# The bound check ahead of the pairs, the first batch's finish a pair earlier, and other moves in a written order

## The chip, the cores and the metric

The kernel runs on one core of a Trainium2 chip. The metric is the device time of one execution in microseconds (us); a kernel is judged by the median of its runs. "Clock" is the mean clock that the throttle granted to TensorE over the span, as a share of full speed.

The engines are named as the profile names them: PE is TensorE's matmul side and PEld its weight load, DVE is VectorE, ACT is ScalarE, POOL is GpSimd, SP is SyncE, which in this kernel issues most DMAs. "ACT's queue" or "POOL's queue" are DMAs that those engines issue.

## The reference, cut to what matters

x is 2 x 512 x 64 x 32 in fp32: two images with 512 channels and S = 2048 tokens. Two layers follow one another, all in fp32.

```python
# layer 0: attention over all 2048 tokens, 8 heads of 64
qk = concat([x, freq_and_time_embedding], channels)       # 512 + 64 channels
q, k, v = qk @ Wq, qk @ Wk, x @ Wv
o = softmax(q k^T / 8) v                                   # per head, 2048 x 2048
x1 = o @ Wout + bout + x

# layer 1: Nystroem attention, 256 landmarks, 8 heads of 64
q, k, v = layernorm(x1) @ Wqkv                             # q scaled by 1/8
qL, kL = mean of q, k over groups of 8 tokens              # 256 landmarks
attn1, attn2, attn3 = softmax(q kL^T), softmax(qL kL^T), softmax(qL k^T)
z = attn2^T / (max column sum * max row sum of attn2)      # maxima over all heads and images
6 times: xz = attn2 z; z = z (13 - xz (15 - xz (7 - xz))) / 4
t = x1 + (attn1 (z (attn3 v)) + conv33(v)) @ Wout + bout   # conv over 33 tokens, per head
out = t + layernorm(t) @ W_nf4^T @ W^T                     # W_nf4: 4-bit weights, dequantised
```

Note the scale of z: it needs attn2 of every head and image, so no pseudo-inverse can begin before the last head's attn2 is there.

## The kernel before, in words

**Who sets the order.** The program is one function, fast_path, under a manual schedule: PE, DVE, ACT and POOL each carry out their instructions in the order in which the Python code emits them. Only SP's queue is ordered by the scheduler. Overlap is made by emitting pieces of one piece of work between pieces of another: such a piece of work is a generator, `advance(gens, n)` takes n steps from a list of generators, and a step that yields GAP takes a turn without emitting anything (the next generator in the list gets the turn instead). So the place of each `yield` and each `gap(n)` is a place in the engines' queues. A token block is 512 tokens, four per image; channels are four chunks of 128.

**Opening.** Twenty warm-up matmuls (L848) keep PE busy while the first weights, the embedding and x arrive. The class Heads0 prepares a pair of heads of layer 0: for queries and for keys a small matmul makes the embedding's part (frequency row plus time row), one 128 x 2048 addition on POOL (L889) sums the two into an e tile, and the projections (L902) are evicted with e added (L905).

**Layer 0.** attention0 handles eight pairs of heads one after the other, four per image. Per group of steps it emits scores (L1066), exps (L1074), additions of the exps (L1084) and values (L1096). Beside it run generators that make the next pair's keys, queries and values, and, during the first pairs of the second image, finish0_units for the first image: per token block an output projection with residual (L965, evicted in L972), a mean over channels by matmul (L987, from L984), a subtraction (L988), squares on ACT (L991, L994), additions on DVE (L996, L997), a variance matmul (L1000), a square-root (L1002) and the normalised block, written to DRAM as x_hat. At the end of an attention a loop runs until the one generator that the next attention needs is finished:

```python
            if not group:
                while needed in filler:
                    advance(filler)
```

`advance(filler)` takes the steps from the front of the list, so other generators in it run too, until the needed one is done.

**Layer 1, first pass.** keys_and_queries (L1239) projects x_hat; per pair, attend makes attn2 (the landmark products L1280 and their exps L1287) for its two heads, and gram (L1307) the start of the pseudo-inverse. In all pairs but the last, attend's two heads share one score tile, sc2, of two banks: the exp of the first head reads it before the second head's product writes its own half. Sixteen small memsets of ones columns (L1275) run on POOL. After the last pair's attend, start_scale (L1191 to L1196) makes zs, the common scale of all pseudo-inverses.

**Layer 1, second pass.** A loop runs over eight pairs, `todo`: the four of image 1, then the four of image 0. In each of its turns pinv of the pair runs, with three others woven into it. The pseudo-inverse of both heads is five iterations of flips (L1522, transposes) and products (L1532) with DVE subtractions (L1545), then three narrow products ending in u (L1507, L1516). After each iteration `chunk(c)`, c = 0 to 4, is called, and six times in the end part `last(i)`. In chunk(c), c = 0 to 3, stand

- attn1 of the pair before, token block c: scores (L1589), exps (L1594), the sum of the two exps (L1598), values in PSUM bank av1 (L1605), row sums over partitions (attn1_sums: matmuls L779 into rs and an ACT copy L1613), the inverse (attn1_inverse: DVE reciprocal L1618 and `spread`, eight SP DMAs, L790, that bring rinv to all partitions), and, one chunk later, the end: av1 times rinv on DVE (L1625), added into o on POOL (L1626);
- attn3 of the pair after, steps 2c and 2c + 1: scores (L1361), exps (L1370), additions (L1375), values (L1382).

chunk(4) has the 33-tap convolution of the next pair (L1459), and the values of the pair after that (L950) go into the `last` steps.

**Finish of layer 1.** Finish1 handles one token block: its x1 comes back from DRAM by four SP loads of 256 KB (L1637); then the output projection (L965, evicted in L972), statistics as above, a DVE reciprocal of the deviation (L1650), the folded feed-forward map mT (L1682), its scaling and residual (L1671, L1672) and a store (L1673). For image 1, finish1_units is a generator over four blocks; it is put into the list `finish` when the loop's fifth turn (n == NPAIR) has ended, and its steps are taken wherever chunk and last call `advance(finish)`. All its blocks share one xr buffer, xb_g, so a block's load waits for the stores of the block before.

**Tail.** After the loop, attn1 of the last pair (last_attn1), what remains of image 1's finish and the first two blocks of image 0's finish are emitted by a string with one letter per step:

```python
    for c in "f1f1f1f1f1f1f1fa1a1a1as11bs1bs1bbt":
```

f is a step of image 1's finish, 1 of last_attn1, a and b of the two blocks' output projections, s and t of their statistics. Then comes the bound check: a matmul bp_f (L2058) of a half-and-half matrix, halves_f, set by three POOL memsets (L2054 to L2056), small DVE operations and an all-reduce over partitions on POOL (L2064). Its flag decides, after the fast path, whether a general path runs instead. The feed-forward maps fp_g of image 0's four blocks (L1682) follow; wide_banks puts them alternately into product banks and the side banks av1 and av3.

Of the kernel before, what the change touches and what calls it, by code (L numbers as in the profile page):

```python
# [663 lines left out]
def fast_path(  # L664
# [157 lines left out]
    nc.vector.memset(emb_sb, 0.0)  # L822
# [3 lines left out]
    def load_w0(kind, cols, queue=nc.sync):  # L826
        w = {"q": wq0, "k": wk0}[kind]
        nc.sync.dma_start(w_sb[kind][:, :, cols], chunked(w[:C, cols]))
        queue.dma_start(we[kind][:, cols], w[C:, cols])

    nc.gpsimd.dma_start(emb_sb[:32, :H], freq)
    nc.gpsimd.dma_start(emb_sb[32:, H:], time)
    load_w0("q", slice(0, P), nc.scalar)

# [23 lines left out]
    class Heads0:  # L858
# [12 lines left out]
        def embedded_and_projected(self, kind):  # L871
# [5 lines left out]
            def embedded(kind):  # L877


                e = wpool0.tile([P, H, W], F32, tag="e", name=f"e_{kind}_{self.name}")  # L880
                flat, kept = e.rearrange("p h w -> p (h w)"), e_d["qk".index(kind), self.hp]
                if self.b:
                    nc.sync.dma_start(flat, kept)
                    return flat
                fp = bank(f"fp_{kind}_{self.name}")
                nc.tensor.matmul(fp[:, : H + W], lhsT=we[kind][:, cols], rhs=emb_sb, start=True, stop=True)
                ft = wpool0.tile([P, H + W], F32, tag="ft", name=f"ft_{kind}_{self.name}")
                nc.vector.tensor_copy(ft, fp[:, : H + W])
# [91 lines left out]
    def statistics(xb, xn, part, name, squares, row):  # L980
# [73 lines left out]
    def attention0(hd, filler, n_filler, needed, beside=None, every=False):  # L1054
# [62 lines left out]
        for i in range(0, len(steps) + 1, GROUP):  # L1117
# [13 lines left out]
            if not group:  # L1131
                while needed in filler:
                    advance(filler)
# [74 lines left out]
    class Pair:  # L1208
# [419 lines left out]
    class Finish1:  # L1628
# [13 lines left out]
        def steps(self, row):  # L1642
# [5 lines left out]
            for rstd in statistics(self.xb, self.xn, self.xn[:, :2, :], self.name, squares, row):  # L1648
# [236 lines left out]
    todo[1].prefetch_w()  # L1885
    vals = [values(1)]
    advance(vals)
    for n in todo[NPAIR - 1].front():
        advance(vals, n // 2)
    start_scale()  # L1890
    todo[0].prefetch1(kvpool.tile([P, S], F32, tag="k", name="q2_first"))
# [4 lines left out]
    for n, pair in enumerate(todo):  # L1896
# [122 lines left out]
    fs = [last_block(t) for t in range(NTB)]  # L2019

# [5 lines left out]

    outs = [f.out_units() for f in fs]
# [9 lines left out]
    st = [f.steps(deviation_of(t)) for t, f in enumerate(fs)]  # L2037

    ones_last = last_attn1()
    for c in "f1f1f1f1f1f1f1fa1a1a1as11bs1bs1bbt":  # L2040
        if c == "f":
            advance(finish)
        else:
            next({"1": ones_last, "a": outs[0], "b": outs[1], "s": st[0], "t": st[1]}[c])
# [5 lines left out]

    n = 3 * B * NPAIR

    halves = row_of("halves_f")[:, :P]
    nc.gpsimd.memset(halves, 0.0)  # L2054
    nc.gpsimd.memset(halves[:D, :D], 1.0)
    nc.gpsimd.memset(halves[D:, D:], 1.0)  # L2056
    bp = bank("bp_f")
    nc.tensor.matmul(bp[:, :n], lhsT=halves, rhs=bound, start=True, stop=True)  # L2058
    ok = small.tile([P, n], F32, name="ok_f")
    nc.vector.tensor_scalar(ok, bp[:, :n], SAFE, None, ALU.is_lt)  # L2060
    oks = small.tile([P, 1], F32, name="oks_f")
    nc.vector.tensor_reduce(oks, ok, AX.X, ALU.min)
    nc.vector.tensor_scalar(oks, oks, -1.0, 1.0, ALU.mult, ALU.add)
    nc.gpsimd.partition_all_reduce(bad, oks, P, bass_isa.ReduceOp.max)  # L2064

# [99 lines left out]
```

## Time and profile before

| | |
|---|---|
| median of 3 runs | 2764.85 us (2764.79 to 2766.75) |
| the profiled execution's own time | 2763.73 us |
| its span | 2761.9 us |
| granted clock, mean | 0.995 |
| layer 0's scores (L1066), first to last start | 55.0 to 1377.3 us |
| layer 1's keys and queries (L1239), first to last start | 1280.8 to 1727.5 us |
| zs ready, first flip of the second pass | 1741.2 us, 1746.3 us |
| HBM traffic | 90.87 MB read, 63.57 MB written |

The profile is of one execution, and its span lies 1.8 us inside that execution's own time; the runs' median is another 1.1 us above it. In a busy table each engine has its busy time, its share of the span and its instruction count. In the rows of groups, "out<-in" names the tiles written and read, and what follows the bar is busy time, mean duration of one in ns, and idle time just ahead of the group with its releaser. A row of the waits has the waiting instruction, its releaser, then total us, number and longest single wait. In a timeline, a row is start, duration, engine, line and operation, with the wait ahead of it in brackets. A row of the stretch table has the stretch, its length, busy time of PE, PEld, DVE, ACT and POOL with instruction counts, granted clock, DMA share and GB/s.

### The profile page before, as it was taken

The page shows a single profiled execution, that of the slowest core. Times are in us where ns is not written, and L with a number is a line of the kernel's source. Part 1 is how long each engine was busy: PE and PEld are TensorE (multiplying, and loading weights), DVE is VectorE, ACT ScalarE, POOL GpSimd, SP SyncE. Part 2 cuts the span into 40 slices and gives each one's busy share as a digit, 9 for nine tenths or more (in the row PEclk, how much of TensorE's full clock was granted, in tenths as well). Part 3 has the DMA queues.
Part 4 walks back from the last instruction along what each step waited for, and adds up shares of the span by engine and source line. Part 5 has one row for each costly group of instructions (what it writes and reads, how often), then busy time and mean ns, then how long its engine had stood idle before and what let it go on. Part 6 is the DMA issues. An engine that isn't in the chain of part 4 may idle for free. (4 is left out here: it accounts for less than half of the span.)

```text
span 2761.9 us, 41236 instructions
## 1 busy us (share of the span) xinstructions
PE 2703.8 (98%) x16994; PEld 1363.3 (49%) x16994; DVE 1629.0 (59%) x2068; ACT 905.8 (33%) x1352; POOL 164.7 (6%) x125
## 2 busy tenths in 40 slices
PE   9999999999999999999999999999999999899898
PEld 5343443434443334343344465777667767555334
DVE  2768787765558756657657444544644545556465
ACT  1434343433335334344512222223332323221210
POOL 1101101000001100000011000000000000000000
PEclk9999999999999999999999999999999999999999
DMA  4100000212111210021035532213111202111301
GB/s 145 42 9 24 28 20 26 83 35 69 32 66 54 96 39 9 21 73 41 24 107 187 187 121 90 95 32 126 43 36 59 81 9 90 40 64 31 107 31 47
DMA packets 112661, 174.00 MB, mean 63 GB/s; under 512 B 16320, under 2 KB 68048, under 8 KB 107856
## 3 DMA queue, kind: packets, MB, share of 16 engines
q1 hardware_dynamic: 107968, 154.46, 17.3%
q0 software_dynamic: 4416, 16.79, 1.6%
q8 instruction: 135, 2.21, 0.3%
q14 instruction: 62, 0.51, 0.1%
q10 hardware_dynamic: 80, 0.03, 0.0%
HBM read 90.87 MB, written 63.57 MB: 56 GB/s over the span
## 5 line engine op out<-in xcount | busy, mean ns | idle before, releaser
L1084 DVE TENSOR_TENSOR acc_f<-acc_f,p_f 128x1024 f32<-128x1024 f32 x448 | 582.6, 1300 | 208.8 <-ACT p_f L1074 180.2
L1074 ACT ACTIVATE p_f<-sc_f 128x1024 f32<-128x1024 f32 x512 | 496.4, 1021 | 564.2 <-PE sc_f L1066 561.5
L1066 PE MATMUL sc_f<-q_f,k_f 64*64 64x512 f32 x4096 | 491.1, 594 | 2.7 <-ACT p_f L1074 2.7
L1096 PE MATMUL av_f<-p_f,v_f 64*64 64x512 f32 x4096 | 484.3, 589 | 0.0
L1096 PEld LDWEIGHTS av_f<-p_f,v_f 64*64 64x64 f32 x4096 | 156.5, 133 | 283.0 <-issue 283.0
L1066 PEld LDWEIGHTS sc_f<-q_f,k_f 64*64 64x64 f32 x4096 | 145.8, 133 | 285.6 <-issue 262.0
L1239 PE MATMUL pp<-xh,w 128*128 128x512 f32 x512 | 231.0, 603 | 0.7 <-ACT q L1242 0.7
L1239 PEld LDWEIGHTS pp<-xh,w 128*128 128x128 f32 x512 | 95.8, 192 | 122.2 <-issue 115.0
L1532 PE MATMUL pb<-R 128*128 128x192 f32 (+1 forms) x640 | 151.1, 383 | 1.6 <-DVE M L1545 1.6
L1532 PE MATMUL pa<-M 128*128 128x192 f32 (+1 forms) x640 | 150.7, 380 | 0.1
L950 PEld LDWEIGHTS vp_f<-wv_f,x 128*128 128x128 f32 x1024 | 115.7, 192 | 13.5 <-issue 11.8
L950 PE MATMUL vp<-w,xh 128*128 128x128 f32 x1024 | 120.8, 276 | 0.0
L950 PEld LDWEIGHTS vp<-w,xh 128*128 128x128 f32 x1024 | 117.0, 192 | 7.2 <-issue 4.2
L1532 PEld LDWEIGHTS pb<-R 128*128 128x128 f32 x640 | 107.7, 192 | 25.1 <-DVE M L1545 2.3
L950 PE MATMUL vp_f<-wv_f,x 128*128 128x128 f32 x1024 | 118.7, 277 | 0.0
L1532 PEld LDWEIGHTS pa<-M 128*128 128x128 f32 x640 | 108.0, 193 | 21.0 <-ACT M L1523 2.5
L902 PE MATMUL pp_q_f<-x,wq_f 128*128 128x512 f32 x256 | 114.4, 599 | 2.1 <-DVE q_f L905 1.4
L965 PE MATMUL yp_g<-o,wo_f 128*128 128x512 f32 x256 | 115.5, 598 | 0.8 <-DVE y_g L1671 0.8
L902 PE MATMUL pp_k_f<-x,wk_f 128*128 128x512 f32 x256 | 114.3, 599 | 1.7 <-DVE k_f L905 1.3
L1682 PE MATMUL fp_g<-xn_g,mT 128*128 128x512 f32 (+1 forms) x264 | 115.7, 589 | 0.0
L965 PE MATMUL yp_f<-q_f,wo_f 128*128 128x512 f32 x256 | 113.7, 598 | 0.9 <-DVE xr_f L972 0.9
L1114 POOL TENSOR_TENSOR q_f<-q_f,rinv_f 128x512 f32<-128x512 f32 x32 | 44.4, 1387 | 1041.9 <-DMA rinv_f<-acc_f 850.7
(196 smaller groups left out, 2719.3 us busy)
## 6 DMA issues: line engine op xcount, KB each, us to landing
xh<-xh_fd SPq DMA_DIRECT2D x12, 1024.0 KB, 5.6
rinv_f<-acc_f SPq DMA_DIRECT2D x256, 32.0 KB, 1.8
xr_f<-in_x_dram SPq DMA_DIRECT2D x8, 1024.0 KB, 5.2
x_fd<-xr_f POOLq DMA_DIRECT2D x8, 1024.0 KB, 5.0
xh_fd<-xn_f POOLq DMA_DIRECT2D x8, 1024.0 KB, 4.6
k_fd<-k SPq DMA_DIRECT2D x32, 256.0 KB, 2.6
q_fd<-q SPq DMA_DIRECT2D x32, 256.0 KB, 3.1
xb_g<-x_fd SPq DMA_DIRECT2D x32, 256.0 KB, 4.2
```

Source lines behind the costliest of these rows:

```text
L902: nc.tensor.matmul(pp, lhsT=w_sb[kind][:, k, cols], rhs=xbs[t][:, k, :], start=k == 0, stop=k == KC - 1)
L950: nc.tensor.matmul(vp[:, j * P : (j + 1) * P], lhsT=xb[:, k, j * P : (j + 1) * P], rhs=w_of(k), start=k == 0, stop=k == KC - 1,)
L965: nc.tensor.matmul(yp, lhsT=wo_sb[:, k, m * P : (m + 1) * P], rhs=oTs[k][:, toks], start=k == 0, stop=k == NPAIR - 1,)
L1066: nc.tensor.matmul(sc[r * D : (r + 1) * D, h, :], lhsT=hd.k[rows, lo : lo + D], rhs=hd.q[rows, t * TB : (t + 1) * TB], start=True, stop=True,)
L1074: nc.scalar.activation(p, sc, AF.Exp, scale=D**-0.5)
L1084: nc.vector.tensor_tensor(acc, first if c == 1 else acc, p, ALU.add)
L1096: nc.tensor.matmul(av[r][half, :], lhsT=hd.v[keys, c, half], rhs=pp[keys, h, :], start=c == 0, stop=c == NST - 1,)
L1114: nc.gpsimd.tensor_tensor(o, o, rinv, ALU.mult)
L1239: nc.tensor.matmul(pp, lhsT=self.w[j][:, c, :], rhs=xhs[t][:, c, :], start=c == 0, stop=c == KC - 1)
L1532: nc.tensor.matmul(dst, lhsT=lhsT[:, k, t * P : (t + 1) * P], rhs=rhs[:, k, :], start=k == 0, stop=k == 1)
L1682: nc.tensor.matmul(fp[:, cols], lhsT=mT[:, k, m * P : (m + 1) * P], rhs=self.xn[:, k, cols], start=k == 0, stop=k == KC - 1,)
```

## The change

It has nine parts, all moves of work that was there before, apart from a second score tile and a few instructions cut differently.

1. *Opening.* The embedding tile is cleared in two small pieces. The embedding's two loads and the first query weights go to ACT's queue. The first pair's two e sums run on DVE instead of POOL.
2. *statistics* can yield between the ACT squares and the DVE additions (`apart`).
3. *finish0_units* has one gap more ahead of the first block.
4. *attention0.* The loop at the end of an attention advances the needed generator alone; other generators are advanced only when it takes a GAP, and otherwise run on in the next attention.
5. *attend.* Each head gets a score tile of its own; the memsets of ones go to DVE.
6. *Bound check.* The memsets, the matmul, the DVE operations and the all-reduce go to the place around start_scale, ahead of the second pass.
7. *Finish of image 1.* A block's x1 comes by one 1 MB load on POOL's queue, issued two finish steps ahead of its first use; the gaps inside norm_units are placed otherwise; and the generator joins `finish` in chunk(1) of the fifth turn, not at its end.
8. *Chunk.* attn1's row sums come after both of attn3's value steps, not between them.
9. *Tail.* last_attn1 emits a block's addition right after its second exps, and the order string is another one; "n" makes the last image's blocks, whose loads are issued there.

```diff
-    nc.vector.memset(emb_sb, 0.0)
+    nc.vector.memset(emb_sb[:32, H:], 0.0)
+    nc.vector.memset(emb_sb[32:, :H], 0.0)
...
-        nc.sync.dma_start(w_sb[kind][:, :, cols], chunked(w[:C, cols]))
+        queue.dma_start(w_sb[kind][:, :, cols], chunked(w[:C, cols]))
...
-    nc.gpsimd.dma_start(emb_sb[:32, :H], freq)
-    nc.gpsimd.dma_start(emb_sb[32:, H:], time)
     load_w0("q", slice(0, P), nc.scalar)
+    nc.scalar.dma_start(emb_sb[:32, :H], freq)
+    nc.scalar.dma_start(emb_sb[32:, H:], time)
...
-                nc.gpsimd.tensor_tensor(
+                engine = nc.gpsimd if self.b or self.hp else nc.vector
+                engine.tensor_tensor(
                     e,
...
-    def statistics(xb, xn, part, name, squares, row):
+    def statistics(xb, xn, part, name, squares, row, apart=False):
...
             nc.scalar.activation(other, xn[:, 2 + i * n : 2 + (i + 1) * n, :], AF.Square)
+        if apart:
+            yield
+        for i, other in enumerate(others):
             to = sq[:, i * n : (i + 1) * n, :]
             nc.vector.tensor_tensor(to, to, other, ALU.add)
...
             nc.sync.dma_start(xb, chunked(x[b])[:, :, t * TB : (t + 1) * TB])
-            yield from gap()
+            yield from gap(1 if t else 2)
...
                 while needed in filler:
-                    advance(filler)
+                    own = [needed]
+                    if not advance(own):
+                        advance(filler)
+                    if not own and needed in filler:
+                        filler.remove(needed)
...
-            scs = scores_bank(f"sc2_{i}") if i + 1 < NPAIR else None
+            scs = [scores_bank(f"sc2_{i}_{h}")[:, 0, :] for h in range(2)] if i + 1 < NPAIR else None
...
-                nc.gpsimd.memset(X[h][:, :, LM:], 1.0)
+                nc.vector.memset(X[h][:, :, LM:], 1.0)
...
-                sc = scs[:, h, :] if scs is not None else bank(f"sc2_{i}_{h}")
+                sc = scs[h] if scs else bank(f"sc2_{i}_{h}")
...
-        def __init__(self, b, t, os, xb, xn):
+        def __init__(self, b, t, os, xb, xn, t_by_t=False):
...
+            if t_by_t:
+                nc.gpsimd.dma_start(xb, chunked(x1_d[b])[:, :, toks])
+                return
...
         def norm_units(self):
-            steps = self.steps(lambda: deviation(self.name))
+            steps = self.steps(lambda: deviation(self.name), True)
+            next(steps)
+            yield from gap(2)
+            next(steps)
+            yield
             next(steps)
             yield GAP
-            next(steps)
-            yield
             next(steps)
             yield from gap(2)
             next(steps)
...
-            f = Finish1(b, t, os, xb, lambda: block_of(lpool, "xn", f"xn_g_{b}_{t}"))
+            f = Finish1(b, t, os, xb, lambda: block_of(lpool, "xn", f"xn_g_{b}_{t}"), True)
+            yield from gap(2)
             yield from f.out_units()
...
     advance(vals)
     for n in todo[NPAIR - 1].front():
         advance(vals, n // 2)
+    n_bounds = 3 * B * NPAIR
+    bp = bank("bp_f")
+    nc.tensor.matmul(bp[:, :n_bounds], lhsT=halves, rhs=bound, start=True, stop=True)
+    ok = small.tile([P, n_bounds], F32, name="ok_f")
+    nc.vector.tensor_scalar(ok, bp[:, :n_bounds], SAFE, None, ALU.is_lt)
...
     start_scale()
+    nc.gpsimd.partition_all_reduce(bad, oks, P, bass_isa.ReduceOp.max)
...
         def chunk(c):
...
+            if n == NPAIR and c == 1:
+                finish.append(finish1_units(1, [p.o for p in todo[:NPAIR]]))
             advance(finish)
...
-            if ones_before:
-                before.attn1_sums(c)
             if after:
                 after.attn3_values(2 * c + 1)
             if ones_before:
+                before.attn1_sums(c)
                 before.attn1_inverse(c)
...
         pair.pinv(chunk, last)
-        if n == NPAIR:
-            finish.append(finish1_units(1, [p.o for p in todo[:NPAIR]]))

     def last_attn1():
         pair, ended = todo[-1], []
+        pair.attn1_add(0)
...
                 if ended:
                     pair.attn1_end(ended.pop())
+                if j:
+                    pair.attn1_add(t)
                 yield
-            pair.attn1_add(t)
             pair.attn1_values(t)
...
-    for c in "f1f1f1f1f1f1f1fa1a1a1as11bs1bs1bbt":
+    for c in "11ffnf11f1ff1afafff1f1f1f1faas11bs1bs1bbt":
```

The bound check's old place after the order string is gone; its memsets of halves_f stand ahead of the matmul in the new place too.

More of the change, by code (lines that the diff above doesn't have):

```diff
@@ L1640, in out_units, with steps @@
             return residual_units(self.b, self.t, self.xb, self.os, wo_sb, b1_sb, self.name)
-        def steps(self, row):
+        def steps(self, row, apart=False):
             def squares():
@@ L1647, in steps @@
             self.xn = self.xn()
-            for rstd in statistics(self.xb, self.xn, self.xn[:, :2, :], self.name, squares, row):
+            for rstd in statistics(self.xb, self.xn, self.xn[:, :2, :], self.name, squares, row, apart):
                 if rstd is not None:
@@ L1885, in fast_path @@
     todo[1].prefetch_w()
+    halves = row_of("halves_f")[:, :P]
+    nc.gpsimd.memset(halves, 0.0)
+    nc.gpsimd.memset(halves[:D, :D], 1.0)
+    nc.gpsimd.memset(halves[D:, D:], 1.0)
     vals = [values(1)]
@@ L1889, in fast_path @@
         advance(vals, n // 2)
+    n_bounds = 3 * B * NPAIR
[3 more added lines that the diff above has]
+    nc.vector.tensor_scalar(ok, bp[:, :n_bounds], SAFE, None, ALU.is_lt)
+    oks = small.tile([P, 1], F32, name="oks_f")
+    nc.vector.tensor_reduce(oks, ok, AX.X, ALU.min)
+    nc.vector.tensor_scalar(oks, oks, -1.0, 1.0, ALU.mult, ALU.add)
     start_scale()
+    nc.gpsimd.partition_all_reduce(bad, oks, P, bass_isa.ReduceOp.max)
     todo[0].prefetch1(kvpool.tile([P, S], F32, tag="k", name="q2_first"))
@@ L2016, in last_block @@
         return Finish1(0, t, [p.o for p in todo[NPAIR:]], xb, xn)
-    fs = [last_block(t) for t in range(NTB)]
     def turns(units, *others):
@@ L2025, in turns @@
         drain(units)
-    outs = [f.out_units() for f in fs]
     def deviation_of(t):
@@ L2034, in deviation_of @@
         return row
-    st = [f.steps(deviation_of(t)) for t, f in enumerate(fs)]
     ones_last = last_attn1()
-    for c in "f1f1f1f1f1f1f1fa1a1a1as11bs1bs1bbt":
+    for c in "11ffnf11f1ff1afafff1f1f1f1faas11bs1bs1bbt":
         if c == "f":
             advance(finish)
+        elif c == "n":
+            fs = [last_block(t) for t in range(NTB)]
+            outs = [f.out_units() for f in fs]
+            st = [f.steps(deviation_of(t)) for t, f in enumerate(fs)]
         else:
-            next({"1": ones_last, "a": outs[0], "b": outs[1], "s": st[0], "t": st[1]}[c])
+            next(ones_last if c == "1" else {"a": outs[0], "b": outs[1], "s": st[0], "t": st[1]}[c])
     assert not finish
@@ L2049, in fast_path @@
     next(st[0])
[L2051 to L2064, printed above, removed]
     for t in range(NTB):
```

## The prediction, made before the changed kernel ran

> **What bounds the kernel now.** I read the page's busy table and its 40 slices first, then the waits of PE, then a table of ten-microsecond stretches, then the timeline around each long wait.
>
> ```profile
> PE 2703.8 (98%) x16994; PEld 1363.3 (49%) x16994; DVE 1629.0 (59%) x2068; ACT 905.8 (33%) x1352; POOL 164.7 (6%) x125
> ...
> PE   9999999999999999999999999999999999899898
> ...
> PEclk9999999999999999999999999999999999999999
> ```
>
> TensorE is the bound nearly everywhere, and the change removes no matmul. So all there is to win is PE's idle time, 2761.9 - 2703.8 = 58.1 us, and what the clock loses after idle stretches. The waits of PE say where it lies:
>
> ```profile
> PE p_pb L1522 <- DVE R L1545: 7.2, 2, 6.8
> PE sc L1280 <- ACT X L1287: 6.2, 3, 3.5
> PE rs L779 <- DVE acc L1598: 5.1, 1, 5.1
> PE bp_f L2058 <- POOL halves_f L2056: 4.9, 1, 4.9
> PE mean_g L987 <- DVE xn_g L984: 3.0, 1, 3.0
> ...
> PE wp L1507 <- DVE R L1545: 2.4, 2, 1.6
> ```
>
> The third number is the longest single wait. Most of these are one event each, and every one is at a place that the change touches. In the stretch table, idle after 2300 us is 24.5 us up to 2660 and 5 us around 2664; from 1740 to 2300 PE waits 1.8 us in all. The clock column adds a second loss:
>
> ```profile
> 1490.00:1500.00 10.00, 6.91 (x14) 3.13 (x14) 9.76 (x18) 4.03 (x6) 4.26 (x4) 0.83 0.39 145
> ```
>
> 0.83 over 10 us is 1.7 us of full-speed work lost. The same 0.83 stands at 1530, 2520, 2590 and 2660; 2380 and 2390 have 0.91 and 0.75 (3.4 us). Seven stretches: 11.9 us, 6.8 of it between 2300 and 2660.
>
> [...] The trace agrees on the halving (eight matmuls took 5.23 us after a 3.47 us wait, 3.70 elsewhere), but a wait of 2.02 us (at 1530.8) was followed by it too, so I count waits of 2 us and more. [...] the trace's loads take 1.28 us. [...] POOL's 1 MB stores landed after 4.6 and 5.0 us here. I take 5 us.
>
> **The change part by part.**
>
> *Opening.* The first head's two embedding sums go from POOL (3.62 us each, the first starting only at 12.84) to DVE. The nearest row is L988's 128x2048 subtraction, 2.29 us. PE then loses neither 0.94 us (17.24, queries' eviction late) nor most of 1.33 us (33.62, keys'): the key sum reuses a buffer whose store to DRAM ended near 29.1, so it ends near 31, the eviction at 31.6, and about 0.6 of the 1.33 stays. The 0.45 us of one SP issue saved brings the second x block (0.6 us wait) forward by perhaps 0.2. The warm-up matmuls run until 8.0 and cover the embedding and weight loads on ACT's queue (four issues of about 0.5 us, landing 3 to 4 us later). The two small memsets cost nothing behind the same warm-up. Together -1.8 (bounds -2.8 and 0).
>
> *Layer-0 finish.* The last block's mean and variance move out of the stretch where only the next queries are projected, into the next attention. Gone: 1.40 us (919.55, mean) and 0.73 us (935.0, exp behind the table load). New: the scores must wait about 0.3 us for the last query eviction, which the variance used to cover; in the attention a square-root between two table loads holds ACT 1.28 + 0.69 + 1.28 = 3.25 us where two groups need an exp within about 2 us of slack (0.5), and the squares (2.1 us) 0.3. The gap before its first block costs nothing: other units fill it. -1.0 (-2.1 to +1).
>
> *attend.* The two halves get a score tile each, so the second product no longer waits for the first exp.
>
> ```profile
> 1488.49 1.13 PE L1280 MATMUL sc<-L,L 64*128 64x256 f32 x4
> ...
> 1493.09 1.24 PE L1280 MATMUL sc<-L,L 64*128 64x256 f32 x4 [3.47 <-ACT X L1287]
> ...
> 1494.26 5.23 PE L1239 MATMUL pp<-xh,w 128*128 128x512 f32 x8
> ...
> 1496.15 0.69 DVE L997 TENSOR_TENSOR xr_f<-xr_f 128x512 f32<-128x512 f32 x1
> ...
> 1499.34 1.02 PE L1000 MATMUL var_n<-xr_f,mean_w 128*128 128x512 f32 x2
> ```
>
> Here the wait does not vanish: PE would reach the variance at about 1494.4, but DVE, busy 9.76 of these 10 us, ends its squares at 1496.84. So the variance runs at 1496.9 instead of 1499.3: 2.4 of 3.47, and the slow clock probably stays. The wait of 2.02 us at 1530.8 goes whole, as X is normalised (1535) before the Gram product needs it (1537), and its 1.7 of clock goes too; the one of 0.7 goes. The sixteen memsets (two of 128x2 for each of eight pairs), now on DVE, are under 0.1 us each, hidden behind the exps. -6.8 (-9.6 to -4).
>
> *Bound check.* It leaves the tail for the place before the pairs. There one matmul, three small DVE operations (0.45 us) and a second all-reduce (0.38) lengthen the path to zs by about 1 us; M was ready for its first use at about 1742, the flip at 1746.3 comes 3 us later, so nothing. The final copy of the flag waits there on POOL too, inside that slack. In the tail:
>
> ```profile
> 2661.65 0.69 DVE L1625 TENSOR_TENSOR rinv<-av,rinv 128x512 f32<-128x512 f32 x1 [0.36 <-DMA rinv<-acc]
> ...
> 2664.31 0.40 PE L2058 MATMUL bp_f<-bound,halves_f 128*128 128x24 f32 x2 [4.95 <-POOL halves_f L2056]
> ```
>
> What is late next: fp_g of the last batch writes bank av1 (wide_banks), which this DVE multiplication reads until 2662.3. PE, free at 2659.4, still waits 3 us. So 2.2 of the 4.95 + 0.25 goes, and the clock's 1.7 stays. -2.2 (-6.9 to 0).
>
> *Batch 1's finish, started a pair earlier, loads on POOL two steps ahead.* In the old order:
>
> ```profile
> 2386.12 1.75 SPq L1637 DMA_DIRECT2D xb_g<-x_fd  x4
> ...
> 2389.65 0.75 DVE L972 SCALAR_TENSOR_TENSOR xb_g<-yp_g,b_f,xb_g 128x512 f32<-128x512 f32 x1 [10.39 <-DMA xb_g<-x_fd]
> ...
> 2390.85 0.48 PE L1522 MATMUL p_pb<-ident,R 128*128 128x128 f32 x1 [6.76 <-DVE R L1545]
> ```
>
> The block's load waits for the previous block's output (behind a spread on SP), DVE waits for the load, pinv waits for DVE. All stalls of 2300 to 2660: 24.5 us, and 6.8 of clock, 31.3. In the new order I walk PE and DVE with the rows' durations and find these left or new: 2.0 where the sixth pair begins (squares of 2.2 us stand on ACT before its first flip, and no filler does); 1.5 in its third chunk (3.25 us of table loads and root on ACT, a 3.34 us reciprocal on DVE); 2.9 and 1.7 of clock in the eighth pair's first chunk, where block 2's load is asked for at the chunk's start: output landing 2.4, load 5, eviction at +9.7, reciprocal 1.75 and R behind it, PE wanting R at +10.1 and getting it at +13; 1.1 twice in its third chunk and before its last iteration; 1.1 in its last steps (table load, one product behind R); 1.5 at var_g of block 3 (squares and a reciprocal before it); 1.5 elsewhere. That is 13.3, with a second clock loss of 1.7 about 15. Gone: 16 (bounds 4 to 29). The POOL queue's blocked load has only the adds of o behind it, read a pair later or blocks later.
>
> *Row sums behind both value products.* rs comes one group of eight matmuls (1.08 us) later in 23 chunks, with the ACT copy, the 1.75 us reciprocal and eight SP issues behind it. In the chunk at 1950, rinv was multiplied at 1966.91 without a wait, and DVE then idled 1.80 us; the next writer of that bank, av at 1969.77, has 2.17 us in hand. 1.08 fits: 0 (0 to +10).
>
> *Tail order, loads of the last batch:* same instructions; counted above.
>
> **Sum**, against this profiled execution (2763.73 us, span 2761.9): -1.8 - 1.0 - 6.8 - 2.2 - 16 = -27.8, so 2735.9; the median of the runs shown is 1.1 above it: 2737.
>
> **The rivals.**
> - *Likeliest, 0.60:* as summed; 2737, own range 2727 to 2747.
> - *Clean order, 0.20:* the stalls that I walked into the finish are mostly covered, 27 gone of 31.3, and attend's clock loss goes too (8.5). 1.8 + 1.3 + 8.5 + 2.2 + 27 = 41: 2724. For it: idle before is a few single events. Against: each needs DVE and ACT on time in chunks that gain work.
> - *The stalls move, 0.14:* finish work inside attn3's chunks makes ACT's table loads and DVE's reciprocals late there; the finish returns only 4. 12 + 4 = 16: 2749. For it: three-microsecond blocks on in-order engines; against: those chunks' DVE is half idle.
> - *Slower, 0.03:* the spread, 1.08 us later, lands after av needs its bank. The first 2.17 us cost nothing. In 23 chunks, 27.8 + 5.5 us are lost once each pays 1.45 us, so when rinv comes 3.6 us later than now; at 4 us it is 1.83 x 23 = 42, giving 2779. Against: nothing but 1.08 is in sight.
> - *No change, 0.03:* idle only changes place, within 0.2% (5.5 us, about what a measurement of this kernel can tell from none): 2765.
>
> Faster 0.60 + 0.20 + 0.14 = 0.94, same 0.03, slower 0.03. The range, 2721 to 2753, holds the first case, most of the second and third.
>
> **What would show it.** Right: PE's waits have no sc from X, no p_pb of 6.8, no bp_f; a wait of about 3 us of fp_g on the last rinv; DVE waiting for POOL's load in the eighth pair's first chunk; 1490 still at 0.83, 1530 at 1.00. Wrong: waits of av on rinv in pairs two to five, or a PE idle sum after 2300 above 25 us or below 12.

## The result, and the profile after

| | before | changed |
|---|---|---|
| median of 4 runs each | 2765.80 us (2764.79 to 2768.34) | 2749.45 us (2748.10 to 2750.93) |
| the profiled execution's own time | 2763.73 us | 2750.93 us |
| its span | 2761.9 us | 2749.0 us |

The ratio of the runs is 0.994, with a 95% interval of 0.9926 to 0.9954: 16.4 us less, where 27.8 less was predicted (2737, range 2721 to 2753). The two profiled executions lie only 12.8 us apart, so this pair of traces shows some 3.6 us less than the runs do. The changed kernel's busy table and slices:

```profile
PE 2699.2 (98%) x16994; PEld 1364.5 (50%) x16994; DVE 1629.5 (59%) x2087; ACT 906.9 (33%) x1354; POOL 160.9 (6%) x109
...
PE   9999999999999999999999999999999999998999
```

PE's idle time is 49.8 us, 8.3 less; its busy time is 4.6 less with the same 16994 matmuls. The waits of PE, by length:

```profile
PE p_pb L1533 <- DVE R L1556: 6.2, 3, 3.8
PE rs_f L779 <- DVE acc_f L1090: 6.2, 4, 3.2
PE var_n L1006 <- issue: 3.7, 1, 3.7
PE fp_g L1699 <- DVE rinv L1636: 3.2, 1, 3.2
...
PE var_g L1006 <- DVE sq_g L1003: 1.5, 1, 1.5
```

The waits of sc on X, of rs on acc and of bp_f are gone, and of mean_g's 3.0 us 0.3 is left. Three of these rows stood in the prediction in kind and nearly in size: fp_g on the last rinv (3 said, 3.2), p_pb in the eighth pair (2.9 said, 3.8), var_g of block 3 (1.5 said, 1.5). The row of rs_f did not: before it was 3.0 us in three waits, now there is a fourth of 3.2. The signs that the prediction named for being right are all there, and its signs of being wrong are not: no av waits on rinv in pairs two to five, and PE's idle sum after 2300 us is 20.1, between its 12 and 25.

Where the time changed is best seen by the start of the same instruction in both traces: POOL's multiplication of q_f at the end of token blocks in layer 0, and the scaling of M at each pair's start in the second pass.

| instruction | before | changed | offset |
|---|---|---|---|
| q_f, pair 5 of layer 0, block 3 of 4 | 880.04 | 879.38 | -0.66 |
| q_f, pair 6, block 4 of 4 | 1104.48 | 1108.53 | +4.05 |
| q_f, the last of layer 0 | 1399.00 | 1403.43 | +4.43 |
| M, pair 1 of the second pass | 1741.29 | 1739.04 | -2.25 |
| M, pair 2 | 1829.77 | 1827.07 | -2.70 |
| M, pair 5 | 2120.96 | 2116.43 | -4.53 |
| the end of the last DVE operation | 2755.79 | 2744.74 | -11.05 |

So in these traces layer 0's finish *lost* 4.7 us, where 1.0 of gain was predicted. The first pass won 6.7 (6.8 predicted). Pairs two to four each won 0.6, where nothing was predicted. From pair 5 on 6.5 was won, where the finish and the bound check were to bring 18.2.

### The profile page after: what moved, and what is told of

The parts are those of the page before. It is cut to its first block, busy times and chain, and to the rows that moved or that the text cites. A ratio compares the mean times of both kernels' runs of the same rounds, so it can differ in the third digit from the quotient of the medians.

```text
span 2749.0 us, 41182 instructions
## 1 busy us (share of the span) xinstructions
PE 2699.2 (98%) x16994; PEld 1364.5 (50%) x16994; DVE 1629.5 (59%) x2087; ACT 906.9 (33%) x1354; POOL 160.9 (6%) x109
## 5 line engine op out<-in xcount | busy, mean ns | idle before, releaser
L1090 DVE TENSOR_TENSOR acc_f<-acc_f,p_f 128x1024 f32<-128x1024 f32 x448 | 582.3, 1300 | 215.5 <-ACT p_f L1080 187.3
L953 PEld LDWEIGHTS vp_f<-wv_f,x 128*128 128x128 f32 x1024 | 115.7, 192 | 13.5 <-issue 11.8
```

The source lines that it names most:

```text
L953: nc.tensor.matmul(vp[:, j * P : (j + 1) * P], lhsT=xb[:, k, j * P : (j + 1) * P], rhs=w_of(k), start=k == 0, stop=k == KC - 1,)
L1090: nc.vector.tensor_tensor(acc, first if c == 1 else acc, p, ALU.add)
```

## Experiments

Each experiment takes "the changed kernel" or "the kernel before", as its expectation says, and makes the edit shown. Line numbers are those of the kernel that is profiled, so the same operation can have another number in another kernel. All kernels were timed beside runs of the kernel before; a ratio r stands for r x 2766 us, and its 95% interval, in brackets, reaches 2 to 4 us to either side. A difference of that size between two edited kernels is not told from none.

### The row sums' order alone

```diff
-            if ones_before:
-                before.attn1_sums(c)
             if after:
                 after.attn3_values(2 * c + 1)
             if ones_before:
+                before.attn1_sums(c)
                 before.attn1_inverse(c)
```

> The kernel before with one edit: attn1's row sums behind both of attn3's value steps. The prediction's term, that the order is worth 0: pair starts (M<-A,zs) stay 97.06 us apart in pairs two to five, and the time stays within 0.1%. Theory from the two traces: the eight row-sum matmuls no longer stand between two groups of value matmuls, a chunk from its first attn1 scores to the next goes from 15.47 to about 15.31 us, pair starts 96.45 apart, and 23 chunks give 23 x 0.16 = 3.7 us, so about 2761 where before is 2765 (0.13%). Rival from the prediction (the spread lands too late): av waits on rinv in these chunks and the time rises by up to 10 us.

Measured: 2764.83 against 2766.75, ratio 0.9991 (0.9983 to 0.9999). The pairs' starts stand 96.45 us apart, as in the changed kernel, and 97.07 before. One chunk of the kernel before in the timeline, from the first attn1 scores to the next:

```profile
1950.66 1.99 PE L1589 MATMUL sc<-q,L 64*128 64x512 f32 x8
...
1956.08 1.03 PE L1382 MATMUL av<-p,v 128*64 128x256 f32 x8
1957.04 0.64 PE L779 MATMUL rs<-acc,ones 128*32 128x256 f32 x8
1957.61 1.08 PE L1382 MATMUL av<-p,v 128*64 128x256 f32 x8
1958.62 0.33 PE L1522 MATMUL p_pa<-ident,M 128*128 128x128 f32 x1
...
1966.13 1.99 PE L1589 MATMUL sc<-q,L 64*128 64x512 f32 x8
```

The same chunk with the row sums behind both value steps:

```profile
1951.16 1.99 PE L1589 MATMUL sc<-q,L 64*128 64x512 f32 x8
...
1952.41 0.69 DVE L1625 TENSOR_TENSOR rinv<-av,rinv 128x512 f32<-128x512 f32 x1 [0.39 <-issue]
...
1956.57 1.90 PE L1382 MATMUL av<-p,v 128*64 128x256 f32 x16
1958.40 0.64 PE L779 MATMUL rs<-acc,ones 128*32 128x256 f32 x8
1958.97 0.33 PE L1522 MATMUL p_pa<-ident,M 128*128 128x128 f32 x1
...
1966.47 1.99 PE L1589 MATMUL sc<-q,L 64*128 64x512 f32 x8
```

The chunk takes 15.31 us, not 15.47. From the first value matmul to the next flip it is 2.40 us instead of 2.54: the sixteen value matmuls run as one group in 1.83 us, and not as two groups of 0.96 and 1.01 around the eight row sums. rinv comes later, but DVE idles only 0.39 us ahead of the multiplication with it, and nobody waits for the multiplication. The theory holds in the trace: 23 chunks of 0.15 us give some 3.5. In the runs the medians differ by 1.9, with an interval from 0.3 to 4.7. In this profiled execution the clock lost 18.8 us, against 11.9 in that of before, which hides the gain there (see the last section).

### attend alone

```diff
-            scs = scores_bank(f"sc2_{i}") if i + 1 < NPAIR else None
+            scs = [scores_bank(f"sc2_{i}_{h}")[:, 0, :] for h in range(2)] if i + 1 < NPAIR else None
...
-                nc.gpsimd.memset(X[h][:, :, LM:], 1.0)
+                nc.vector.memset(X[h][:, :, LM:], 1.0)
```

> The kernel before with one edit: attend's score tile for each head and the memsets on DVE. The prediction's term: 6.8 us less (4 to 9.6), with 1490 still at 0.83 clock and the wait moved from sc to var_n, and the stretch at 1530 at full clock. Rival: the DVE queue is the bound there, and less than 4 us comes back, because var_n then waits as long as sc did.

Measured: 2757.48 against 2766.75, ratio 0.9967 (0.9955 to 0.9979), 9.3 less. Pair 1 starts 8.4 us earlier than before. The wait sits where the prediction put it. The profile names no releaser for var_n ("issue"), but the last addition of the squares on DVE ends just ahead of it:

```profile
1495.22 0.69 DVE L997 TENSOR_TENSOR xr_f<-xr_f 128x512 f32<-128x512 f32 x1
...
1496.01 1.10 PE L1000 MATMUL var_n<-xr_f,mean_w 128*128 128x512 f32 x2 [3.69 <-issue]
```

From the first sc to var_n it is 8.46 us, here as in the changed kernel, and 10.85 before: 2.4 us less, as worked out. The clock, though, did not fall at all around this wait (1.00 in both stretches from 1490 to 1510), while in the changed kernel it did after the same wait of 3.69 us (0.83 from 1500 to 1510). So the mechanism and its size in PE's waiting time were right. The forecast kept one clock loss of 1.7 us that is gone in this execution. Whether that makes the 2.5 us by which 9.3 exceeds 6.8, one trace can't say; the last section has what such losses went with in the traces.

### Layer 0: the old loop, and the norm one group later

```diff
-                    own = [needed]
-                    if not advance(own):
-                        advance(filler)
-                    if not own and needed in filler:
-                        filler.remove(needed)
+                    advance(filler)
```

> The changed kernel with one part undone: attention0's end loop as it was, so that the last token block's mean and variance are made beside the next queries again. The prediction's term says that the loop's part gains 1.0, so this would be 1 us slower than the changed kernel (2750). Theory from the trace: the new place of the last norm costs more (rs_f waits 3.2 us for acc_f, 0.86 for an exp, and about 1.7 of clock around 1000 to 1012) than the three waits it removed (0.88 + 1.40 + 0.73), so the offset of +4.8 us that arises between 990 and 1105 goes: about 2745, and no rs_f wait of 3 us near 1008.

Measured: 2742.84, ratio 0.9917 (0.9903 to 0.9930): 6.6 less than the changed kernel. The last q_f of layer 0 stands at 1398.66, 4.8 us before the changed kernel's. The new loop is thus the loss. Why, the changed kernel's timeline shows around the last normalisation, which now falls into an attention:

```profile
998.38 3.35 DVE L1023 RECIPROCAL rstd_n<-rstd_n 128x512 f32<-128x512 f32 x1 [2.05 <-ACT rstd_n L1008]
...
1000.74 2.00 PE L1072 MATMUL sc_f<-q_f,k_f 64*64 64x512 f32 x16 [0.86 <-ACT p_f L1080]
1001.77 1.22 DVE L1026 TENSOR_TENSOR xn_f<-xn_f,rstd_n 128x1024 f32<-128x1024 f32 x1
1001.82 3.39 POOL L1025 TENSOR_TENSOR xn_f<-xn_f,rstd_n 128x1024 f32<-128x1024 f32 x1 [24.23 <-DVE rstd_n L1023]
...
1002.91 4.71 DVE L1090 TENSOR_TENSOR acc_f<-acc_f,p_f 128x1024 f32<-128x1024 f32 x2
...
1007.67 0.64 PE L779 MATMUL rs_f<-acc_f,ones 128*32 128x256 f32 x8 [3.21 <-DVE acc_f L1090]
```

A token block of the attention ends just here, so its row sums rs_f need the last additions into acc_f. These stand on DVE behind the reciprocal and the multiplication, and then take 4.71 us for two, where two take 2.56 alone. The extra time is the first one's: it begins while POOL multiplies and ends 1.08 us after POOL does, 3.38 us instead of 1.23. If that is the cause, moving this step, the reciprocal and the two multiplications, behind those additions must win the loss back with the new loop kept:

```diff
             next(last)
             yield
+        yield from gap(1)
         next(last)
```

> The changed kernel (2749.45) with one edit: one more gap ahead of the last token block's reciprocal and normalisation in finish0_units, so that these DVE operations come one group of steps later, behind the last additions of the token block's exps and not ahead of them. Theory: the loss of the new end loop is the wait of rs_f for acc_f (3.2 us) and the clock after it (1.7), because the 3.35 us reciprocal, 1.2 of multiplication and the additions beside POOL's multiplication stand ahead of acc_f on DVE; both go, 4.9 less, about 2744.5, nearly as good as with the old loop (2742.8). Rival: the loss sits in the table loads (0.86 for the exp) and in the displaced fillers; then under 1.5 us comes back.

Measured: 2742.81, ratio 0.9917 (0.9904 to 0.9931), 6.6 less than the changed kernel. The additions run at once, rs_f starts without a wait, and the exp's wait of 0.86 is still there:

```profile
1000.89 2.56 DVE L1091 TENSOR_TENSOR acc_f<-acc_f,p_f 128x1024 f32<-128x1024 f32 x2 [4.38 <-ACT p_f L1081]
1000.91 2.00 PE L1073 MATMUL sc_f<-q_f,k_f 64*64 64x512 f32 x16 [0.86 <-ACT p_f L1081]
...
1004.56 0.64 PE L779 MATMUL rs_f<-acc_f,ones 128*32 128x256 f32 x8
```

The table loads were thus not the loss; the place of one step of the normalisation against the end of a token block was. The experiment moves the step as a whole. By the trace, 2.15 of the 3.21 us that rs_f waited are the addition standing beside POOL's multiplication, and the rest is DVE's queue.

### The finish of image 1 as it was

The edit takes the changed kernel and puts back the finish's four SP loads, norm_units, last_attn1 and the order string of before, and

```diff
-            if n == NPAIR and c == 1:
-                finish.append(finish1_units(1, [p.o for p in todo[:NPAIR]]))
...
         pair.pinv(chunk, last)
+        if n == NPAIR:
+            finish.append(finish1_units(1, [p.o for p in todo[:NPAIR]]))
```

> The changed kernel with the finish of image 1, the places of its gaps, its SP loads and the tail's order string as before; bound check, opening, attend, loop and row sums as changed. The prediction's term: the finish gives 16, so this would be 16 us slower than the changed kernel (2765). Theory from the trace: idle and clock lost from 2120 to 2660 fell by about 8 us only, so this is 7 to 9 us slower (about 2758), and the waits of p_pb (6.8), mean_g (3.0) and rs on acc (5.1) are back. Rival: the bound check's new place, not the finish, gave what was gained there: under 3 us slower.

Measured: 2757.47, ratio 0.9964 (0.9950 to 0.9977): 8.0 slower than the changed kernel. The long waits of before are back:

```profile
PE p_pb L1533 <- DVE R L1556: 9.3, 3, 8.2
...
PE rs L779 <- DVE acc L1609: 5.0, 1, 5.0
...
PE mean_g L990 <- DVE xn_g L987: 3.0, 1, 3.0
```

The finish's new place, loads and order are worth 8, not 16. It is the theory of the two traces that holds here, not the prediction's term. Which of the four moves (the earlier start, the gaps, the one load on POOL's queue, the order string) gives the 8 is not separated.

### The bound check alone

The edit moves halves_f, bp_f, ok and the all-reduce ahead of the pairs, in the kernel before, as part 6 of the change does.

> The kernel before with one edit: the bound check ahead of the pairs. The prediction's term: 2.2 less (between 0 and 6.9), the bp_f wait of 4.95 gone, a wait of fp_g of about 3 us on the last rinv multiplication in its place, and the pairs' start not later by over 0.2 us. Rival: the clock after the shorter wait no longer falls, and 4 us come back.

Measured: 2767.11 against 2766.12, ratio 0.9999 (0.9991 to 1.0008). bp_f's wait is gone, and as said fp_g waits in its place:

```profile
2667.63 6.59 PE L1682 MATMUL fp_g<-xn_g,mT 128*128 128x512 f32 x8 [3.12 <-DVE rinv L1625]
```

4.95 became 3.12, and the eight matmuls behind it took 6.59 us, where they took 5.38 before: in this execution half clock lasted 6.8 us there, and 3.4 before. The gain of 1.8 us in waiting is within what the runs leave open; a gain of 2.2 lies inside the interval, as does none.

### What is late next: four edits on the changed kernel with the old loop

Another bank for the first product of the last image:

```diff
-        return product_bank(name) if m % 2 else side_bank(1 + m, name)
+        return product_bank(name) if m % 2 else side_bank(3 - m, name)
```

> The changed kernel with the old end loop (2742.84, loop_back) and one edit: wide_banks gives av3 to chunk 0 and av1 to chunk 2, so that the first fp_g of the last image does not wait for the last rinv multiplication, which reads av1. Theory (the prediction's term for what is late next): the fp_g wait of 3.2 us and the clock of up to 1.7 after it go; about 2738 to 2740. Rival: the last product waits for something else at the same time (rstd's reciprocal or the previous xn), and under 1 us comes back.

Measured: 2740.98, ratio 0.9911 (0.9896 to 0.9927), 1.9 less than loop_back. No wait of fp_g is left; in the trace the last DVE operation ends 5.4 us earlier, while the medians differ by less than the wait's 3.2. The size stays open between 0 and 5; that the bank caused the wait is shown.

A block's projection one step later:

```diff
-            yield from gap(2)
+            yield from gap(3 if t == 2 else 2)
             yield from f.out_units()
...
-    for c in "11ffnf11f1ff1afafff1f1f1f1faas11bs1bs1bbt":
+    for c in "11ffnf11f1ff1afafff1f1f1f1ffaas11bs1bs1bbt":
```

> The changed kernel with the old end loop (2742.84) and one edit: token block 2 of image 1 takes one gap more between its load and its output projection (and one more f in the string). Theory (the prediction's term for the eighth pair's first chunk): the eviction that waits for the load then stands behind pinv's subtractions and not ahead of them, so the p_pb wait of 3.8 us and the half clock after it (3.4 us lost over 6.7 us) go; 5 to 7 us less, about 2737. Rival: every later step is shifted by one, and its waits move to other chunks; within 2 us of 2742.8.

Measured: 2754.23, ratio 0.9962 (0.9948 to 0.9975): 11.4 *slower* than loop_back, where the rival had allowed 2. p_pb's wait of 3.8 is gone (0.7 is left), and the shifted steps brought worse ones:

```profile
PE rs L779 <- DVE acc L1604: 8.0, 3, 6.3
PE pa L1538 <- ACT M L1529: 7.7, 3, 5.0
```

The waits in the finish hang on which step meets which chunk; one gap for one block, with one letter of the order string for it, moved 11 us.

A buffer of its own for that block, in the same order:

```diff
-            xb = block_of(lpool, "xr", f"xb_g_{b}_{t}")
+            if t == 2:
+                xb = as_block(kvpool.tile([P, NST, P], F32, tag="v", name=f"xb_g_{b}_{t}"))
+            else:
+                xb = block_of(lpool, "xr", f"xb_g_{b}_{t}")
```

> The changed kernel with the old end loop (2742.84) and one edit: token block 2 of image 1 is loaded into a buffer of its own (the keys' buffer, which no attn3 uses any more), not into the xr buffer whose last store must land first; no engine's order changes. Theory: the p_pb wait of 3.8 us in the eighth pair's first chunk is the store's landing (about 3 us) ahead of the 1 MB load on DVE's way to pinv's subtraction; the load is asked for 3 us earlier, the wait falls under 1 us, and with the clock after it 4 to 7 us come back: about 2737. Rival: the load of 5 us alone still makes the eviction late, and then the wait stays above 2 us.

Measured: 2736.33, ratio 0.9890 (0.9875 to 0.9905), 6.5 less than loop_back. In the changed kernel the load is asked for by POOL only when the previous block's store has landed, and DVE's eviction waits for it ahead of pinv's subtraction:

```profile
2474.58 0.77 POOL L1649 DMA_DIRECT2D xb_g<-x_fd  x1 [16.56 <-DMA out_dram<-xb_g]
...
2480.34 0.75 DVE L975 SCALAR_TENSOR_TENSOR xb_g<-yp_g,b_f,xb_g 128x512 f32<-128x512 f32 x1 [7.66 <-DMA xb_g<-x_fd]
2481.01 1.74 DVE L1629 RECIPROCAL acc<-acc 128x256 f32<-128x256 f32 x1
2482.66 0.69 DVE L1556 SCALAR_TENSOR_TENSOR R<-M,pa 128x320 f32<-128x320 f32 x2
...
2483.15 0.43 PE L1533 MATMUL p_pb<-ident,R 128*128 128x128 f32 x1 [3.83 <-DVE R L1556]
```

With the buffer, the eviction no longer waits for a load, and p_pb does not wait in that chunk:

```profile
2470.77 0.75 DVE L975 SCALAR_TENSOR_TENSOR xb_g<-yp_g,b_f,xb_g 128x512 f32<-128x512 f32 x1 [2.28 <-PE yp_g L968]
...
2474.96 0.27 PE L1528 MATMUL p_pb<-ident,R 128*128 128x128 f32 x1
```

This settles the cause of the largest wait that the change left: a buffer, not the order and not the length of the load, which are both as they were.

The bounds behind the squares:

```diff
-            nc.vector.tensor_reduce(most[:, :2], big, AX.X, ALU.max)
+            self.big, self.most = big, most
+
+        def bounds(self):
+            big, most = self.big, self.most
+            nc.vector.tensor_reduce(most[:, :2], big, AX.X, ALU.max)
...
         def front(self):
+            self.bounds()
             self.attend()
```

> The changed kernel with the old end loop (2742.84) and one edit: the five small DVE operations that write bound for a pair of heads (2.6 us near 1494, a 128x1 multiplication of 1.59 us among them) come ahead of that pair's attend, behind the squares of the normalisation, and not ahead of them. Theory: var_n waits behind them on DVE, so its wait goes from 3.7 to about 1.1 us; 2.6 less, and up to 1.7 more where the clock fell. Rival: the additions of the squares themselves are held until POOL's multiplication (3.3 us) ends; then the wait stays above 2.5.

Measured: 2742.49, ratio 0.9915 (0.9902 to 0.9929), 0.4 less than loop_back, which is nothing that the runs can tell. The wait of var_n is 2.4 us, not 1.1:

```profile
1487.85 3.32 POOL L1025 TENSOR_TENSOR xn_f<-xn_f,rstd_n 128x1024 f32<-128x1024 f32 x1 [19.32 <-DVE rstd_n L1023]
...
1490.07 2.19 DVE L1002 TENSOR_TENSOR xr_f<-xr_f 128x1024 f32<-128x1024 f32 x1
```

The addition takes 2.19 us where it took 1.21: it begins while POOL still multiplies, and ends 1.09 us after POOL does. Theory and rival each hold for a half: 1.3 us of the wait went.

### Together

> The changed kernel with the old end loop, the other bank for chunk 0 of the last image, the buffer of its own for block 2, and the bounds behind the squares. If the gains add (1.9 and 0.4 as measured for two of them, 4 to 7 for the buffer), 2734 to 2737; if a wait moves on to the next late work, about 2740.

Measured: 2730.06 us (2727.43 to 2731.34), ratio 0.9872 (0.9857 to 0.9887): 19.4 less than the changed kernel. The parts measured one by one add up to 15.4 (6.6, 1.9, 6.5 and 0.4); the 4 us above that are no more than the intervals leave open. The profiled execution is the fastest of the four, and up to PE's last matmul the clock lost 1.7 us in it, 10.2 in the changed kernel's. Its waits begin with

```profile
PE rs_f L779 <- DVE acc_f L1090: 3.0, 3, 1.2
PE sc_f L1072 <- ACT p_f L1080: 2.7, 8, 0.7
PE var_n L1006 <- issue: 2.4, 1, 2.4
```

so no single wait of over 2.4 us is left behind the opening.

## Why the prediction held in direction and missed in size

- **Opening**, -1.8 predicted, -0.9 in the traces; no run has it alone. The e sums on DVE removed the queries' wait of 0.94, as said. The keys' wait, of which 0.6 was to stay, stayed whole: 1.33 before and 1.77 in the changed kernel, 1.4 on average in the eight profiles with the new opening that are counted here. e_k's sum still starts only when e_q's store has landed, at 29.91 us now and 29.21 before. The second q_f multiplication of layer 0 starts on average at 138.4 us in these eight profiles and at 139.3 in three with the old opening (one of each kind, in which the clock fell during the opening, is left out).
- **Layer-0 finish**, -1.0 predicted with a bound of +1: wrong in sign, +4.7 in the trace and +6.6 in the runs. The two waits that it counted as gone, 1.40 and 0.73, did go. The step that failed is the one that priced the new place: it counted ACT's 3.25 us between table loads (the trace shows 0.86 of wait for them) and left out DVE's reciprocal and multiplication, POOL's multiplication and the addition that stands beside it, though a token block's row sums wait for just that queue. norm_later shows it.
- **attend**, -6.8 predicted: -6.7 in the trace of the changed kernel, -9.3 in the runs of attend alone, inside its bounds of -9.6 to -4. Right, in mechanism and in size.
- **Bound check**, -2.2 predicted: the wait that takes its place was right to 0.2 us; the medians of the runs show no gain (1.0 us more), and the interval holds both the predicted gain and none.
- **Row sums**, 0 predicted with bounds 0 and +10, -1.9 measured: the gain was excluded without a reason. The step asked only whether rinv comes too late, which it does not, and not what the row sums cost where they stood.
- **Finish**, -16 predicted, -8.0 measured. The failed term is what is left or new. The 5 us for a 1 MB load on POOL's queue was the author's estimate; the four loads of xb_g landed after 5.6 us in the changed kernel (median). The waits that the prediction lists add up to 12.7, and with the two clock losses that it names to 16.1; its "about 15" leaves out the 1.1 of the last steps. Measured in the changed kernel's trace, from 2218 to 2652, are 18.6 of waits of 0.35 us or more and 5.1 of clock. Most walked places came near: the sixth pair's start 2.1 (2.0 said), var_g 1.5 (1.5), the eighth pair's first chunk 4.3 (2.9), its third chunk 2.9 (2.2 with its last iteration). The 1.5 in the sixth pair's third chunk did not come. What was called "elsewhere", 1.5, is 5.9: the seventh pair's start and first chunks (1.2, 0.66, 0.60, 0.83), yp_g behind xb_g (1.1) and av behind rinv (1.6).

Measured apart, the parts give -0.9, +6.6, -9.3, 0, -1.9 and -8.0, together -13.5, where the whole gave -16.4; the intervals cover the difference. That the whole came to lie inside the range is in part luck: the likeliest case's own range, 2727 to 2747, did not hold it, and attend and the row sums gave 4.4 us more than was said, which made up for part of what layer 0 and the finish fell short.

The rival that came true in part is the third, the stalls move (2749): its total agrees with the measured one, but by luck, as its account left the finish 4 us of gain, where 8 came, and put no loss into layer 0.

## What to carry to other kernels

When work is moved beside other work on engines that work through their queues in order, as DVE did in the changed kernel when an eviction waited 7.66 us for its load and pinv's subtraction stood behind it, price every engine's queue at the exact meeting point, and ask there what the other work needs next from each: here one step of a reciprocal and two multiplications cost nothing that shows one group later, and 6.6 us in front of the additions that close a block. Where a wait is on a load, look first at what the load itself waits for; a free buffer, with the order kept, won 6.5 us where a shifted order lost 11.4. And when a group of small matmuls is moved out from between two like ones, count the change between groups that goes away: 0.15 us a place here, though no run shows whether the change of shape makes it.

## What the runs showed of the hardware that had not been expected

**The starts of half clock lay multiples of 3.413 us apart.** In the traces half clock lasted 3.41 us or a multiple of it up to PE's last matmul (six stretches before, of 3.41 and once 6.83 us), and each such portion cost 1.7 us of full-speed work. The number of portions was not the same for the same instructions: around sc's wait of 3.47 us near 1493 the kernel before lost one, and rows_alone lost two:

```profile
1490.00:1500.00 10.00, 6.58 (x11) 3.24 (x12) 9.83 (x16) 3.94 (x5) 4.25 (x4) 0.66 0.35 133
```

The clock records of the traces show what went with it. In each of the thirteen traces all starts of half clock lie whole multiples of 3.413 us apart (before: 1493.97, 1531.52 and 2388.27 us, the second and third 11 and 262 portions behind the first; changed: 1008.69, 1500.20 and 2483.24 us, 144 and 432 portions). These multiples make a grid of windows, which lay elsewhere against the program in each execution. Take PE's idle time in each window that ran at full clock, from 20 us to the last matmul: all 51 windows with more than 2.00 us of idle were followed by half clock, none with less than 1.81 was, and of the seven between, four were. The same wait of 3.69 us fell into the grid in two ways (a row has the window, its length, PE's busy time with its matmuls, clock, DMA share and GB/s). In the changed kernel 3.0 us of idle lie in one window:

```profile
1496.78:1500.20 3.42, 0.41 (x1) 1.00 0.71 262
1500.20:1503.61 3.41, 3.41 (x5) 0.50 0.56 200
```

In attend_alone the grid cuts it into 1.9 and 1.8, and the clock stays full:

```profile
1490.78:1494.19 3.41, 1.54 (x4) 1.00 0.08 31
1494.19:1497.61 3.42, 1.60 (x4) 1.00 0.94 353
1497.61:1501.02 3.41, 3.41 (x10) 1.00 0.26 89
```

In the same way the two waits of 1.7 and 0.6 us near 2530 lay in one window with 2.1 us of idle in the changed kernel, and in two with 1.25 and 1.0 in loop_back, where no portion followed. At half clock it took less idle: a portion with 0.49 us of it or more was followed by another in all 19 cases, and of 56 with less only one was. The prediction counted every wait of 2 us and more: near in size, but what half clock went with in these traces was the idle time of one window, which the 3.69 us in attend_alone straddled and the two waits near 2530 shared. All this was read from the traces afterwards; no run was made to test it, and what makes the clock fall is not shown.

Up to its last matmul a profile lost between 1.7 us (together) and 18.8 (rows_alone, bound_alone). A wait of 2 to 4 us thus cost its own length here and, as the grid fell, nothing or 1.7 us or more on top (the 3.69 us: nothing in attend_alone, 1.7 in the changed kernel); single profiles can't price it. Part of the scatter between runs is of this size: of bound_alone's runs the fastest, 2762.76 us, has a granted clock of 0.995, and the slowest, 2771.02, one of 0.991.

**Additions on DVE that began beside POOL's work ended 1.08 us after it.** In the changed kernel's trace 23 of the 448 additions into acc_f (L1090) began while a multiplication or sum ran on POOL. Each ended 1.08 us after POOL's operation did, and so took between 1.67 and 4.48 us; the others took 1.23 at most. In all thirteen traces it is the same but for two additions (in that of before 25 of 26 ended 1.08 to 1.09 us after POOL). So the end of such an addition went with POOL's end, whenever it had begun; what holds it is not shown. Not every DVE operation did this: in the changed kernel reductions (L1269) and evictions (L975) that began beside POOL's operation kept their usual 0.41 and 0.75 us.
